# The last two pieces of a mixture-of-experts feed-forward: where the down products of the final slices are issued

## The chip, the cores and the metric

The kernel runs on one NeuronCore of one Trainium2 chip. The metric is the device time of one execution, in microseconds. Before the change the median of three runs was 898.97 us (898.81 to 903.04). The profile is that of one further execution, which took 899.19 us; its records span 897.3 us, so 1.9 us of that time lie outside the span.

## The reference

For 16 batches of 128 tokens, 512 features each, the reference adds a cross attention (32 query heads, 8 key and value heads, head size 16) to the input, and then a feed-forward with 32 experts. A gate picks 8 experts for each of the 2048 tokens, and the feed-forward is

```python
g = jnp.einsum('td,eid->tei', x, w1)
u = jnp.einsum('td,eid->tei', x, w3)
a = jax.nn.silu(g) * u
routed = jnp.einsum('tei,edi,te->td', a, w2, comb)
sh = jax.nn.silu(x @ shared_w1.T) * (x @ shared_w3.T) @ shared_w2.T
out = routed + sh
```

with D = 512 and I = 256, all in float32. Here "up" is the product with w1 or w3, "down" the product with w2.

## The kernel before, in words

Everything up to the experts (attention, the second layer norm, the gate, the shared expert) is left as it is. The routed part sorts the chosen (token, expert) pairs by expert into one long list of 138 slices of 128 rows, numbered 0 to 137. Each expert has a fixed stretch of the list, its capacity (`CAPS`); unused places hold a token number out of bounds, which a transfer skips. A **piece** is one expert's stretch or half of it. The first and the last expert in the list are cut into two pieces each and computed "directly" (`direct`, `up`: four steps, of four matmuls each in the program, one for w1 and one for w3 for each half of I); the experts between them (`fast`) are computed in seven products (`seven`). The last places of the list are these, from the capacities of 448 rows of the last two experts:

| stretch of the list | slices |
|---|---|
| last but one expert in the list ("expert 30") | 131, 132, 133 and the first 64 rows of 134 |
| last expert ("expert 31"), first piece, 192 rows | the last 64 rows of 134, and 135 |
| last expert, second piece, 256 rows of which 248 are computed | 136, 137 |

For a slice `j`, `down(j)` (lines 1714 to 1735) issues the matmuls of the product with w2 into a bank of PSUM, one bank for even slices and one for odd ones. Slice 134 holds rows of two experts, so its matmuls come as two halves of 64 columns, with two weights. One step later `evict(j)` (line 1739) copies the bank on ScalarE, scaled by the gate's weight, into one of four `yw` buffers, and `send` (line 1695) has GpSimd issue an indirect transfer that adds the 128 rows to the output in HBM. Two experts can hold the same token, so the first send of an expert waits until all sends of the expert before it have landed (`add_manual_dep` in `send`, line 1710). A slice with rows of two experts is sent twice: at once for the first expert, and for the second (`token2`) at the head of the next slice's eviction, through the list `waiting`. In this document the two sends of slice 134 are called 134a (expert 30) and 134b (expert 31).

What the engines are given is an order written out by the Python loop over `pieces`. Each step of a piece issues an up product; `tick()` runs the jobs due at that step (evictions, SiLU, products of the gates); and after a step, as many down products are issued as `planned` lists for it, if the slice's time has come: the list `ready_downs` holds pairs of a slice and the step from which it may be issued. A slice joins the list when the piece after its own begins, with a delay `lag`: 3 steps after a fast piece, 1 after a direct one. `many = max(len(ready_downs) - KEPT, 0)` with `KEPT = 1` spreads all but one over the piece's steps. A planned slice that isn't ready goes to the next step. What is left after the last piece is issued in a row. Each engine's queue runs in this order.

Of the kernel before, what the change touches and what calls it, by code (L numbers as in the profile page):

```python
# [46 lines left out]
def tile_xattn_moe(  # L47
# [978 lines left out]
    def experts(ups, in_order, later, products):  # L1026
# [383 lines left out]
        pieces = []  # L1410
# [70 lines left out]
        def block_copies(js):  # L1481


            runs = []
            for q in range(4):
                for j in js:
                    for n, a, b, col in parts(j):
                        if a <= q * Q < b:
                            r, to = j % NB_BUF, col - a
                            last = runs[-1] if runs else None  # L1490
                            if (
                                last
                                and last[0] == q
                                and last[1] == n
                                and last[2] + last[4] == r
                                and last[3] + last[4] * P == to
                            ):
                                last[4] += 1
                            else:
                                runs.append([q, n, r, to, 1])  # L1500
            for q, n, r, to, many in runs:
                for c in range(4):
                    of = blocks[q * Q : (q + 1) * Q, r : r + many, :]
                    of = of.rearrange("p s (k c j) -> p s k c j", c=4, j=Q)[:, :, :, c, :]
                    dst = xnT[n % NTB][c * Q : (c + 1) * Q]
                    at = min(max(to, 0), TB - many * P)
                    dst = dst[:, :, at : at + many * P]
                    dst = dst.rearrange("p k (s t) -> p s k t", t=P)
                    dst = dst[:, :, :, to + q * Q - at : to + (q + 1) * Q - at]
                    on_ACT = c != q or q % 2 == 0  # L1510
                    copy = nc.scalar.copy if on_ACT else nc.vector.tensor_copy
                    yield on_ACT, 1 + many, lambda dst=dst, of=of, copy=copy: copy(dst, of)  # L1512

        def transpose(j):
            nc.vector.transpose(blocks[:, j % NB_BUF, :], xgs[:, j % NG_BUF, 0:D])  # L1515
            weigh(j)
# [51 lines left out]
        def weight_sums(k):  # L1568


            a11, a12, a21, a22 = (
                wup[k % NW][:, :, d : d + 2, ts(i, P)] for i in range(2) for d in (0, 2)
            )
            s1, s2, s4 = (
                late.tile([P, 2, 2, P], F32, tag=name, name=name) for name in ("s1", "s2", "s4")
            )
            sums[k] = s1, s2, a21, s4
            return [
                lambda o=o, a=a, b=b, op=op: nc.vector.tensor_tensor(o, a, b, op)
                for o, a, b, op in (  # L1580
                    (s1, a21, a22, ALU.add),
                    (s2, s1, a11, ALU.subtract),
                    (a21, a11, a21, ALU.subtract),
                    (s4, a12, s2, ALU.subtract),
                )
            ]
# [12 lines left out]
        def token_sums(n):  # L1599


            h = width(n) // 2
            b11, b12, b21, b22 = halves_of(n)
            t1, t2, t4 = (
                late.tile([P, 2, M], F32, tag=name, name=name)[:, :, 0:h]
                for name in ("t1", "t2", "t4")
            )
            tsums[n] = t1, t2, b12, t4
            for out_, a, b in ((t1, b12, b11), (t2, b22, t1), (b12, b22, b12), (t4, b21, t2)):
                yield lambda o=out_, a=a, b=b: nc.vector.tensor_tensor(o, a, b, ALU.subtract)  # L1610
# [142 lines left out]
        def gather_next():  # L1753
            nonlocal n_gathered
            while n_gathered < NS and (n_gathered < NG_BUF or n_gathered - NG_BUF in weighed):
                gather(n_gathered)
                n_gathered += 1
# [8 lines left out]
        def slices_of(n):  # L1766

            end = pieces[n][2]
            return -(-end // P), end // P
# [9 lines left out]
        KEPT = 1  # L1779
        blocks = late.tile([P, NB_BUF, D], F32, name="blocks", bufs=1)  # L1780

        def fast(k):
            return 0 < k < E - 1

        def direct(n):
            banks = {}
            for step in range(4):
                up(n, step // 2, step % 2, banks)
                yield

        def tick():
            nonlocal now
            for f in jobs.pop(now, []):
                f()

        n_copied = n_turned
        ready_downs = []
        for n in range(len(pieces)):
            k = pieces[n][0]
            steps = 7 if fast(k) else 4  # L1800
            ending = n + 1 == len(pieces) or pieces[n + 1][0] > k
            last_piece = len(pieces) - 1

            if n:
                lag = 3 if fast(pieces[n - 1][0]) else 1
                whole = slices_of(n - 1)[1]
                ready_downs += [(j, now + lag) for j in range(n_down, whole)]
                n_down = whole
            many = max(len(ready_downs) - KEPT, 0)
            planned = [(2 * i + 1) * steps // (2 * many) for i in range(many)]  # L1810

            by_PE = range(0)
            if n == 0:
                by_PE = range(n_turned, slices_of(1)[0])
                n_copied = n_turned = slices_of(1)[0]
            on_DVE, on_ACT = [], []
            if ending and fast(k + 1):
                on_DVE += [(4, f) for f in weight_sums(k + 1)]
            if n < last_piece and fast(pieces[n + 1][0]):
                on_DVE += [(3, f) for f in token_sums(n + 1)]  # L1820
            turning = [
                (5, lambda j=j: transpose(j))
                for j in range(n_turned, slices_of(min(n + 3, last_piece))[0])
            ]
            n_turned = max(n_turned, slices_of(min(n + 3, last_piece))[0])
            to_copy = range(n_copied, slices_of(min(n + 2, last_piece))[0])
            n_copied = to_copy.stop
            assert n_turned - to_copy.start <= NB_BUF
            copying = list(block_copies(to_copy))
            if n == 0:  # L1830
                on_DVE += turning[: len(to_copy)]
                del turning[: len(to_copy)]
            on_ACT += [(c, f) for a, c, f in copying if a]
            on_DVE += [(c, f) for a, c, f in copying if not a]
            on_DVE += turning
            dues = [1.0 + 1.5 * planned.count(step) for step in range(steps)]
            done = 0.0
            sides = [(side, sum(c for c, _ in side)) for side in (on_DVE, on_ACT)]
            lefts = [total for _, total in sides]
            for step, _ in enumerate(seven(n) if fast(k) else direct(n)):  # L1840
                tick()
                done += dues[step]
                if step == 1 and by_PE:
                    turn(by_PE)
                for i, (side, total) in enumerate(sides):
                    due = done / sum(dues)
                    if n == 0:
                        due = max(0.0, 2 * due - 1) if i else min(1.0, 2 * due)
                    while side and lefts[i] > total * (1 - due) + 0.01:
                        c, f = side.pop(0)  # L1850
                        f()
                        lefts[i] -= c
                for _ in range(planned.count(step)):
                    if ready_downs and ready_downs[0][1] <= now:
                        down(ready_downs.pop(0)[0])
                    elif step + 1 < steps:
                        planned.append(step + 1)
                gather_next()
                now += 1
            for side, _ in sides:  # L1860
                for _, f in side:
                    f()
                side.clear()
            if ending and k + NW < E:
                load_weights(k + NW, True, False)
# [11 lines left out]
    pieces = [(k, i) for k in range(NTB) for i in range(NI)]  # L1877
    left_over = attention_small()
    experts(pieces[1:], in_order, *left_over)
    left = nc.values_load(  # L1880
        more[0:1, 0:1],
# [63 lines left out]
```

## Time and profile before

| what | value |
|---|---|
| median of three runs | 898.97 us (898.81 to 903.04) |
| profiled execution: its time, its span | 899.19 us, 897.3 us |
| TensorE (PE) busy | 871.5 us, 97% of the span |
| VectorE (DVE), ScalarE (ACT), GpSimd (POOL) busy | 638.9, 641.0, 506.8 us |
| the sends, line 1695 | 150 of them, mean 1619 ns on POOL, 242.8 us in all |
| median from issue to landing of a send | 5.1 us |
| mean TensorE clock granted | 0.993 of full speed |

Times in the timeline count from the start of the span. PE is the matmul side of TensorE, PEld its weight loads, POOLq or SPq the sequencer of an engine. A send's time on POOL is not that of its transfer; the time to landing is listed apart. One matmul of the program stands as two or more matmuls in the trace[...].

### The profile page before, as it was taken

How to read it: one execution, taken by the hardware profiler on the slowest of the kernel's cores; microseconds unless marked ns; L12 is line 12 of the kernel's file. 1: busy time of each engine (PE TensorE's matmuls, PEld its weight loads, DVE VectorE, ACT ScalarE, POOL GpSimd, SP SyncE). 2: the span in 40 equal slices, each digit the busy share in tenths (PEclk: the TensorE clock that was granted, in tenths of full speed). 3: DMA queues.
4: the chain of work that ended last, by engine and by line, in shares of the span. 5: the costliest groups of instructions: out<-in, count | busy, mean ns of one | idle time of the engine just before them, and what ended most of it. 6: DMA issues, size and time to landing. Idle time of an engine off the chain costs nothing. (4 is left out here: it accounts for less than half of the span.)

```text
span 897.3 us, 15744 instructions
## 1 busy us (share of the span) xinstructions
PE 871.5 (97%) x5055; PEld 606.6 (68%) x5055; DVE 638.9 (71%) x1739; ACT 641.0 (71%) x1338; POOL 506.8 (56%) x622
## 2 busy tenths in 40 slices
PE   8999999999899999999999999999999999999993
PEld 4344444555677877778787878787877777777771
DVE  7877768884778767777777777777897777676310
ACT  5888722331989868787989887888896877886531
POOL 3587642575556546555556565656665665644443
PEclk9999999999999999999999999999999999999998
DMA  9111112416578786778787888788877787776443
GB/s 318 39 48 49 50 46 99 149 63 220 165 157 199 156 201 158 173 166 205 168 201 177 187 181 182 180 188 176 213 180 188 202 218 164 162 171 136 85 59 38
DMA packets 59884, 137.28 MB, mean 153 GB/s; under 512 B 12168, under 2 KB 16392, under 8 KB 59792
## 3 DMA queue, kind: packets, MB, share of 16 engines
q0 software_dynamic: 32032, 69.25, 40.3%
q1 hardware_dynamic: 27680, 66.81, 22.0%
q8 instruction: 42, 0.69, 0.3%
q14 instruction: 50, 0.41, 0.2%
q10 hardware_dynamic: 80, 0.13, 0.0%
HBM read 96.71 MB, written 46.73 MB: 160 GB/s over the span
## 5 line engine op out<-in xcount | busy, mean ns | idle before, releaser
L1695 POOL DMA_INDIRECT out_dram<-yw,token x150 | 242.8, 1619 | 226.7 <-ACT yw L1739 134.3
L1512 ACT COPY xnT<-blocks 32x256 f32<-32x256 f32 (+3 forms) x843 | 358.6, 425 | 12.7 <-DVE blocks L1515 0.8
L1723 PE MATMUL y<-wdn,sa 128*128 128x512 f32 (+2 forms) x672 | 259.7, 594 | 0.0
L1615 PE MATMUL p<-xnT,wup 128*128 128x192 f32 (+26 forms) x1152 | 189.6, 311 | 2.8 <-ACT p L1657 2.8
L1432 POOL DMA_INDIRECT xgs<-rows,token x138 | 149.5, 1083 | 68.8 <-DVE own L1524 22.4
L1615 PEld LDWEIGHTS p<-xnT,wup 128*128 128x128 f32 x1152 | 170.3, 191 | 25.9 <-issue 15.4
L1739 ACT ACTIVATE yw<-y,wt 128x512 f32<-128x512 f32 x138 | 94.9, 688 | 107.1 <-PE y L1723 68.3
L1723 PEld LDWEIGHTS y<-wdn,sa 128*128 128x128 f32 (+2 forms) x672 | 96.0, 171 | 73.1 <-issue 70.3
L1615 PEld LDWEIGHTS p<-t,s 128*128 128x128 f32 x768 | 116.6, 191 | 26.5 <-issue 23.0
L1615 PE MATMUL p<-t,s 128*128 128x128 f32 (+26 forms) x768 | 126.6, 310 | 0.9 <-DVE t L1610 0.9
L1515 DVE STREAM_TRANSPOSE blocks<-xgs 128x512 f32<-128x512 f32 x134 | 94.7, 707 | 5.4 <-DMA out_dram<-x 4.9
L1643 DVE TENSOR_TENSOR z<-u,p 128x256 f32<-128x256 f32 (+26 forms) x96 | 48.5, 505 | 41.4 <-PE p L1615 41.2
L1615 PEld LDWEIGHTS p<-t,wup 128*128 128x128 f32 x384 | 59.4, 190 | 19.4 <-issue 12.4
L475 ACT ACTIVATE p<-sc 128x1024 f32<-128x1024 f32 x64 | 62.1, 1023 | 13.7 <-PE sc L465 13.6
L1643 DVE TENSOR_TENSOR u<-u,p 128x256 f32<-128x256 f32 (+26 forms) x48 | 24.4, 509 | 57.5 <-PE p L1615 57.5
L1615 PE MATMUL p<-xnT,s 128*128 128x128 f32 (+26 forms) x384 | 64.3, 310 | 0.0
L1615 PE MATMUL p<-t,wup 128*128 128x128 f32 (+26 forms) x384 | 64.0, 310 | 0.0
L260 PE MATMUL gu<-xnT,sup 128*128 128x512 f32 x128 | 60.7, 616 | 0.7 <-ACT ssl L268 0.7
L1615 PEld LDWEIGHTS p<-xnT,s 128*128 128x128 f32 x384 | 57.2, 191 | 6.1 <-issue 4.5
L1006 POOL TENSOR_SCALAR hq<-slice_q,sq 128x138 f16<-128x138 f16 x32 | 35.2, 1113 | 38.0 <-DVE sq L1314 21.8
L1610 DVE TENSOR_TENSOR t<-xnT,t 128x256 f32<-128x256 f32 (+26 forms) x96 | 48.8, 509 | 0.9
L465 PE MATMUL sc<-qT,kz 32*128 32x512 f32 x256 | 44.2, 639 | 0.5 <-ACT p L475 0.2
(216 smaller groups left out, 1002.0 us busy)
## 6 DMA issues: line engine op xcount, KB each, us to landing
wup<-in_w_dram SPq DMA_DIRECT2D x64, 512.0 KB, 6.1
wdn<-in_w_dram SPq DMA_DIRECT2D x32, 512.0 KB, 4.5
rows<-xn SPq DMA_DIRECT2D x16, 256.0 KB, 2.0
out_dram<-x SPq DMA_DIRECT2D x16, 256.0 KB, 3.0
x<-in_x_dram SPq DMA_DIRECT2D x15, 256.0 KB, 5.8
out_dram<-yw,token POOLq DMA_INDIRECT x150, 5.1
xgs<-rows,token POOLq DMA_INDIRECT x138, 5.0
cTs<-in_cT_dram SPq DMA_DIRECT2D x4, 256.0 KB, 4.5
```

The source lines that it names most:

```text
L260: nc.tensor.matmul(acc, lhsT=sup[:, w, d, ts(i, P)], rhs=xnT[k][:, d, :], start=(d == 0), stop=(d == ND - 1),)
L465: nc.tensor.matmul(scs[j // 2][:, j % 2], lhsT=kzs[b // 4 % 2][rows, b % 4, i, :], rhs=qT[rows], start=True, stop=True, tile_position=(j * ...
L475: nc.scalar.activation(p, sc, AF.Exp, scale=1.0 / HD**0.5)
L1432: nc.gpsimd.indirect_dma_start(out=t, out_offset=None, in_=rows[:, :], in_offset=bass.IndirectOffsetOnAxis(ap=token[:, j : j + 1], axis=0) ...
L1512: yield on_ACT, 1 + many, lambda dst=dst, of=of, copy=copy: copy(dst, of)
L1515: nc.vector.transpose(blocks[:, j % NB_BUF, :], xgs[:, j % NG_BUF, 0:D])
L1610: yield lambda o=out_, a=a, b=b: nc.vector.tensor_tensor(o, a, b, ALU.subtract)
L1615: nc.tensor.matmul(acc[:, i, 0:h], lhsT=w[:, i, d, :], rhs=x[:, d, :], start=(first and i == d == 0), stop=(i == d == 1), skip_group_check ...
L1643: soon(lambda: nc.vector.tensor_tensor(out_, a, b, ALU.add))
L1695: ins = nc.gpsimd.indirect_dma_start(out=flat, out_offset=bass.IndirectOffsetOnAxis(ap=token2[:, k - 1 : k] if a else token[0:b, j : j + 1 ...
L1723: nc.tensor.matmul(y[c0:c1, :], lhsT=acts[n % NTB][:, i, col : col + c1 - c0], rhs=wdn[pieces[n][0] % NW][:, i, :], start=(i == 0), stop=( ...
L1739: nc.scalar.activation(yws[j], y, AF.Copy, scale=wt[:, j : j + 1])
```

## The change

Three edits, all in the loop over the pieces:

```diff
-                lag = 3 if fast(pieces[n - 1][0]) else 1
+                lag = 3 if fast(pieces[n - 1][0]) else 0
...
-            many = max(len(ready_downs) - KEPT, 0)
+            many = max(len(ready_downs) - KEPT, 0) if n < last_piece - 1 else 0
...
+                if n >= last_piece - 1:
+                    planned += [step] * 2
                 for _ in range(planned.count(step)):
+                    if n == last_piece and len(ready_downs) == 1:
+                        break
                     if ready_downs and ready_downs[0][1] <= now:
                         down(ready_downs.pop(0)[0])
```

The slices of a direct piece may be issued from the first step of the next piece. In the last two pieces nothing is spread: each step may issue two slices, and those it can't issue are passed to the next step on top of that step's own two. In the last piece one ready slice is held back until after the piece.

The order of down products (by slice) and up steps on TensorE becomes:

| | before | after |
|---|---|---|
| behind the last step of piece 31, first half | 131, 132 | 131, 132, 133 |
| behind step 0 of the last piece | nothing | 134 |
| behind step 1 | 133 | nothing |
| behind steps 2 and 3 | nothing | nothing |
| after the pieces | 134, 135, 136, 137 | 135, 136, 137 |

The number of matmuls, evictions and sends is the same, and so is the order of the sends among themselves. On ScalarE the eviction of 133 moves ahead of the first SiLU of the last piece, and that of 134 ahead of the second. Nothing moves on VectorE, GpSimd and SyncE, and nothing anywhere ahead of piece 31.

## The prediction

> **What bounds the kernel now.** The page gives TensorE 97% of the span, so I first asked whether the change takes work from it. It doesn't: the same matmuls run in another order. So the end of the program decides, and I read the chain that ended last, in order of time (start, length, what):
>
> ```profile
> 885.84 0.41 issue
> 886.25 2.66 POOLq L1941
> 888.90 0.30 issue
> 889.21 1.57 POOL out_dram L1695
> ```
>
> The chain ends on GpSimd, not on TensorE, with the 150th send. The timeline of the last 20 us (start, length, engine, operation, count, idle time before it and what ended it) says how it gets there:
>
> ```profile
> 876.46 7.29 PE L1723 MATMUL y<-wdn,sa 128*64 128x512 f32 x20
> ...
> 879.48 1.44 POOL L1695 DMA_INDIRECT out_dram<-yw,token  x1 [3.74 <-ACT yw L1739]
> ...
> 880.40 0.69 ACT L1739 ACTIVATE yw<-y,wt 128x512 f32<-128x512 f32 x1 [1.19 <-PE y L1723]
> ...
> 882.12 0.69 ACT L1739 ACTIVATE yw<-y,wt 128x512 f32<-128x512 f32 x1 [1.03 <-PE y L1723]
> ...
> 883.60 1.56 POOL L1695 DMA_INDIRECT out_dram<-yw,token  x1 [2.68 <-DMA out_dram<-yw,token]
> 883.83 0.69 ACT L1739 ACTIVATE yw<-y,wt 128x512 f32<-128x512 f32 x1 [1.03 <-PEq L1886]
> 885.47 1.57 POOL L1695 DMA_INDIRECT out_dram<-yw,token  x1 [0.30 <-issue]
> 887.34 1.56 POOL L1695 DMA_INDIRECT out_dram<-yw,token  x1 [0.30 <-issue]
> 889.21 1.57 POOL L1695 DMA_INDIRECT out_dram<-yw,token  x1 [0.30 <-issue]
> ```
>
> In the first line slices 134 to 137 run in a row and TensorE ends at 883.75. The sends are 134a (879.48), then 134b (883.60) after 2.68 us idle for a transfer, then 135, 136, 137, each 1.87 us after the one before (1.57 and 0.30 of issue). Slices 135 and 136 were evicted by 881.1 and 882.8, yet went out at 885.47 and 887.34: they stood behind 134b, and 134b stood for the landing of 134a. That landing is in the view of the sends that start between 879 and 880 us:
>
> ```profile
> DMA to landing us min/median/max: 3.3/3.3/3.3
> ```
>
> So 134a lands at 879.48 + 3.3 = 882.78, and 134b starts 0.82 us later. The other landings, looked up likewise, are 4.8, 6.2, 5.0 and 3.3 us from the start of 134b, 135, 136, 137: the last falls at 889.21 + 3.3 = 892.5. After the sends comes line 1941, the end of the program (count, shortest/median/longest in ns, first and last start in us):
>
> ```profile
> L1941 SPq EVENT_SEMAPHORE  x12: 27/28/28, 888.4 to 893.0; - x12
> ...
> L1941 POOLq DRAIN  x1: 10247/10247/10247, 886.2 to 886.2; - x1
> ...
> L1941 ACTq DRAIN  x1: 80/80/80, 887.7 to 887.7; - x1
> ```
>
> SyncE has seen all landings by 893.0, ScalarE and TensorE are through at 887.8, and GpSimd's drain runs to 886.25 + 10.25 = 896.5, which is 5.7 us after the last send ended (890.78) and 4.0 after the last landing (892.5). Only 0.8 us of barrier follow to 897.3. The end thus hangs on the last send, and the last send on the landing of 134a.
>
> **What the Trainium skill says.** "Perfetto Trace Analysis", section "DMA Instruction — SWDGE (GPSIMD)": the profiled end of such a send is the end of descriptor generation, and the movement of data lies outside it. This trace agrees: 1.57 us on POOL, 3.3 to 6.2 us to landing. "DMA: Bandwidth & Descriptors", section "Rules for kernel authors": an accumulating transfer has to wait for the semaphore of an earlier one to the same bytes. The wait of 134b is of that kind, 2.68 us idle here. The same page, section "Anatomy of one DMA — SWDGE (gpsimd) path", gives about 2.0 us fixed per transfer, mostly the confirmation of the write; the sparse send 134a took 3.3 us here, so I use the trace's number.
>
> **The change, step by step.** A full down product takes 4 trace matmuls of 0.43 us, 1.72 us (871.30 to 873.02 for slice 133). Two up steps of the last piece take 16 trace matmuls, 3.34 us (867.96 to 871.30), so one takes 1.67. Slice 134 takes 1.87 (876.46 to 878.33), with 0.10 ahead of it: the up steps before it took 3.44 instead of 3.34.
>
> *TensorE.* The first point that differs is behind slice 132; 131 starts at 864.52. After: 131 to 133 take 3 × 1.72 = 5.16, to 869.68; step 0 takes 1.67, to 871.35; with the 0.10, 134 starts at 871.45 and ends its issue at 873.32; three up steps take 5.01, to 878.33. Then comes 135, and it starts at 878.33 in the trace of before too. So TensorE's end stays; the edit costs nothing there unless a moved product waits. Slice 134 needs the bank of 132 (evicted by about 868.9), the activations of piece 31's first half (last product on VectorE at 864.79 + 0.35 = 865.14) and expert 31's w2 (its load was issued at 849.61; the page's median to landing is 4.5 us): 2.6 us or more of slack in each. Slice 136 needs the last gate product, 878.33 + 0.17 + 0.41 = 878.9 by the pattern at 876.47 to 877.05; held-back 135 covers it until 880.05. Without that cover 136 would start some 0.6 us late.
>
> *ScalarE.* An eviction starts about 0.2 to 0.35 us after its product and takes 0.69. The one of 133 now stands ahead of the first SiLU (869.88 to 870.57; the SiLU's input is ready at 871.4), the one of 134 ahead of the second (873.5 to 874.2; input ready at 876.7). Neither holds a SiLU up: cost nothing. The buffers they write belong to sends 129 and 130, issued at 858.82 and 861.79 and landed by about 865.
>
> *GpSimd.* A send starts 0.96 us after its eviction starts if the engine is free (866.44 to 867.40, and 878.52 to 879.48). 131 and 132 stay at 867.40 and 869.26; 133 comes at 871.13. 134a: eviction at 871.45 + 2.06 (876.46 to 878.52 before) = 873.5, send at 874.46, landing 3.3 later at 877.76, and 134b 0.82 later at 878.6, done at 880.15: wholly beneath the last up steps. 135: evicted from 880.40 as before, sent at 880.40 + 0.96 = 881.36. 136: the later of 882.12 + 0.96 = 883.08 and 881.36 + 1.87 = 883.23. 137: the later of 884.79 and 883.23 + 1.87 = 885.10.
>
> | | before | after, estimate |
> |---|---|---|
> | 134b starts | 883.60 | 878.6 |
> | last send starts | 889.21 | 885.10 |
> | last send ends | 890.78 | 886.67 |
> | POOL's drain ends (+5.7) | 896.5 | 892.4 |
> | span | 897.3 | 893.2 |
>
> The gain is 4.11 us: 2.24 us in which 135 stood for the landing of 134a, and 1.87 for 134b itself in front of it. What is late next is the chain 135's product, eviction, three sends; 137's own eviction would allow 884.79, only 0.31 earlier. Against the profiled execution's 899.19 that is 895.1; the median of the runs lies 0.22 lower, so I forecast 898.97 − 4.1 = **894.9 us**.
>
> *The unknown.* The trace doesn't show what the drain of GpSimd waits for. If for the last send, it moves by 4.11. If for the last landing, it moves by what the landings move: with 135 no longer behind a fresh transfer, 136 takes 4.7 to 5.3 (the pair at 867.40 and 869.26 showed these) and lands at 887.9 to 888.5, 137 at 885.10 plus 2.8 to 3.3 (2.8 is the shortest of the tail), 887.9 to 888.4, so the last landing is at 887.9 to 888.5 against 892.5: a gain of 4.0 to 4.6. I take 4.1, and keep 3.8 and 4.8. A loss is excluded unless a landing grows, below.
>
> **The rivals.**
> *The same chain, worth more.* The landings come early as just worked out, and TensorE saves 0.1 to 0.3 us on fewer waits between banks: a gain of 4.5 to 5.0, near 894.3. For it: four sends in a row before had landings up to 6.2 us, so contention was there. Against: with the drain tied to the send, nothing of it counts.
> *The wait is only shortened.* 134a now goes out 3.3 us behind 133 and may land late. With 6.2 us, the longest of this tail, 134b starts at 874.46 + 6.2 + 0.82 = 881.48 and the last send at 887.09: a gain of 2.1, 896.9 us. Against: up to 4.2 us nothing is lost, and 134a is short of rows (9 GB/s in its slice of the trace, against 119 for 133).
> *The other side.* The same wait, longer: the last send starts at 874.46 + L + 0.82 + 3 × 1.87 = 880.89 + L, with L the landing of 134a. From L = 8.3 the change loses; at L = 13 it costs 4.7, 903.7 us. No landing in the tail is beyond 6.2.
> *It does nothing.* GpSimd's drain is held by something that doesn't move, and the time stays at 899.0. Against: no other engine has anything left after 887.8 but SyncE's waits for these landings.
>
> **How the numbers follow.** About 0.5% (4.5 us) is what a measurement of this kernel can tell from no change, and my 4.1 lies close beneath. The main case has 0.62, with its own range 894.3 to 895.4, and 0.12 of it beyond the line; worth more 0.24; shortened 0.05; nothing 0.04; slower 0.05. Faster by over 0.5%: 0.12 + 0.24 = 0.36. Within: 0.50 + 0.05 + 0.04 = 0.59. Slower: 0.05. The range 893.8 to 896.9 takes the main case, most of the larger one and the shortened one, and leaves out the last two and the tail of the second.
>
> **What would show it.** In the profile after: 134b starts near 878.6 and ends before the last products; no idle time for a transfer ahead of 135; the last three sends at about 881.4, 883.2 and 885.1; TensorE's last down products from 878.3 to 883.7; the drain's end 5.7 us after the last send. I am wrong if 134 starts much after 871.5 (a moved product waits), if 134b still starts after 880, or if the drain's end doesn't follow.

## The result, and the profile after

The changed kernel takes 894.98 us in the median of 17 runs; the kernel before, in 17 runs beside them, 899.99. The measured ratio, which is not the plain quotient of these two medians (0.9944), is 0.9949 with a 95% interval of 0.9935 to 0.9962; a second measurement on another occasion gave 0.9959 (0.9940 to 0.9978). The forecast was 894.9 us. One run of the changed kernel took 2306.47 us and is left out of the ratio, and the other runs of each kernel fall into two groups 3 to 4 us apart (one run of before, 899.99, lies between); the medians of the faster groups are 898.88 and 894.79 us, 4.09 us apart.

The profiled executions took 899.19 us (span 897.3) and 894.69 us (span 892.9), 4.5 us apart; of these 0.37 us lie ahead of the first point where the two programs differ, since slice 131 starts on TensorE at 864.52 before and at 864.15 after. To keep such offsets out (among the executions below they reach 4 us, as much as the gain itself), most times of this section are also counted from the start of slice 131.

First the timeline of the changed kernel, the lines that answer to those of before:

```profile
871.07 1.94 PE L1723 MATMUL y<-wdn,sa 128*64 128x512 f32 x8
...
874.09 1.44 POOL L1695 DMA_INDIRECT out_dram<-yw,token  x1 [1.78 <-ACT yw L1739]
...
878.06 5.31 PE L1723 MATMUL y<-wdn,sa 128*128 128x512 f32 x12
878.17 1.56 POOL L1695 DMA_INDIRECT out_dram<-yw,token  x1 [2.65 <-DMA out_dram<-yw,token]
...
880.03 0.69 ACT L1739 ACTIVATE yw<-y,wt 128x512 f32<-128x512 f32 x1 [3.06 <-PE y L1723]
...
880.99 1.56 POOL L1695 DMA_INDIRECT out_dram<-yw,token  x1 [1.25 <-ACT yw L1739]
...
882.86 1.56 POOL L1695 DMA_INDIRECT out_dram<-yw,token  x1 [0.30 <-issue]
883.46 0.69 ACT L1739 ACTIVATE yw<-y,wt 128x512 f32<-128x512 f32 x1 [1.03 <-PEq L1890]
884.73 1.57 POOL L1695 DMA_INDIRECT out_dram<-yw,token  x1 [0.30 <-ACTq L1890]
```

Slice 134 now runs at 871.07, and 134a goes out at 874.09. GpSimd still idles 2.65 us for its landing ahead of 134b (878.17), about as long as before (2.68), but TensorE is still at work then: 135 to 137 start at 878.06. When 135 has been evicted, 134b is out, and what ended the 1.25 us of idle time ahead of 135 is its own eviction. The wait for the transfer was not removed; it was moved beneath TensorE.

The chain that ended last, for the same stretch (start, length, what), shows it in order; the last three sends in it are those of the timeline:

```profile
874.09 3.30 DMA out_dram<-yw,token
...
878.17 1.56 POOL out_dram L1695
879.74 1.02 issue
...
884.73 1.57 POOL out_dram L1695
```

The landing of 134a took 3.30 us. The chain counts nearly all of the time between 879.74 and 880.99 as issue; the timeline names the wait for 135's eviction there. Less the 0.30 us that lie between any two sends in a row, this is the slack of the transfer, 0.95 us. The end of the program (line 1945 in the changed file, columns as before):

```profile
L1945 SPq EVENT_SEMAPHORE  x12: 28/28/28, 882.8 to 888.7; - x12
...
L1945 POOLq DRAIN  x1: 6530/6530/6530, 885.5 to 885.5; - x1
```

GpSimd's drain ends at 885.48 + 6.53 = 892.01, which is 5.72 us after the last send's end (886.29), as before (890.78 to 896.50, 5.72).

| from the start of slice 131 | before | after | difference |
|---|---|---|---|
| 134a starts | 14.96 | 9.94 | 5.02 |
| 134b starts | 19.08 | 14.02 | 5.06 |
| 135 sent | 20.95 | 16.84 | 4.11 |
| last send starts | 24.69 | 20.58 | 4.11 |
| TensorE ends | 19.23 | 19.23 | 0.00 |
| drain of GpSimd ends | 31.98 | 27.86 | 4.12 |

### The profile page after: what moved, and what is told of

Its sections match the earlier page's. It is cut to its first block, busy times and chain, and to the rows that moved or that the text cites. A ratio compares the mean times of both kernels' runs of the same rounds, so it can differ in the third digit from the quotient of the medians.

```text
span 892.9 us, 15745 instructions
## 1 busy us (share of the span) xinstructions
PE 872.7 (98%) x5055; PEld 608.4 (68%) x5055; DVE 639.3 (72%) x1739; ACT 640.9 (72%) x1338; POOL 505.4 (57%) x622
## 4 chain that ended last, share of the span: by engine, by line
PE 93%; issue 2%; POOL 1%; ACT 1%; DVE 1%; DMA 1%; POOLq 0%; ACTq 0%; DVEq 0%
PE p L1615 44%; PE y L1723 25%; PE gu L260 6%; PE sc L465 5%; PE oT L481 3%; PE y L1348 3%; PE x L435 2%; PE gu L1546 2%; POOL out_dram L1695 1%; PE tok L1012 1%; DMA out_dram<-yw,token 1%; PE warm L331 1%; PE lgT L542 0%; PE lg L557 0%; ACT p L475 0%
## 5 line engine op out<-in xcount | busy, mean ns | idle before, releaser
L1432 POOL DMA_INDIRECT xgs<-rows,token x138 | 146.8, 1063 | 70.3 <-issue 25.4
```

The source lines that it names most:

```text
L1432: nc.gpsimd.indirect_dma_start(out=t, out_offset=None, in_=rows[:, :], in_offset=bass.IndirectOffsetOnAxis(ap=token[:, j : j + 1], axis=0) ...
```

## The experiments

Two theories on the gain. **W**, that of the prediction: the end hangs on GpSimd's chain of sends, and the gain is the wait for 134a's landing plus the slot of 134b. **T**: the new order on TensorE is worth the time by itself. And on what closes the program: **S**, the drain follows the last send; **L**, it follows the last landing; **P**, it follows whatever GpSimd did last.

### Slice 134 one step later

```diff
-                lag = 3 if fast(pieces[n - 1][0]) else 0
+                lag = 3 if fast(pieces[n - 1][0]) else 1
```

> The changed kernel with the delay of a direct piece back at 1 step, so that slice 134 is issued behind step 1 of the last piece instead of step 0, 1.67 us later on TensorE; all else as changed. Times on the scale of the changed kernel's trace (slice 131 starts at 864.15, last send at 884.73, span 892.9). Theory W (the end hangs on the chain 134a, its landing, 134b, 135, 136, 137): 134a starts at 874.09 + 1.67 = 875.76, lands 3.3 later, 134b starts at 879.84 and leaves GpSimd free at 881.70; 135 starts there instead of at 880.99, so 0.71 us of the 1.67 come through, the last send starts at 885.44 and the span is 893.6. Rival T (the gain comes from TensorE, whose down products now stand in fewer, longer rows): TensorE ends where it did, the span stays at 892.9 within 0.2.

Measured: span 892.6, time 894.32 (one run). GpSimd's lines:

```profile
875.46 1.44 POOL L1695 DMA_INDIRECT out_dram<-yw,token  x1 [3.45 <-ACT yw L1739]
878.80 1.56 POOL L1695 DMA_INDIRECT out_dram<-yw,token  x1 [1.90 <-DVE sa L1560]
880.69 1.56 POOL L1695 DMA_INDIRECT out_dram<-yw,token  x1 [0.33 <-ACT yw L1739]
```

134a comes 1.67 us later as expected (11.61 from the start of slice 131). But 134b follows it after 3.34 us where it took 4.08 in the changed kernel and 4.12 before. The timeline puts the end of 134b's idle time down to an operation of VectorE that was over at 878.44; the chain of this execution has the landing of 134a there, 2.55 us after its start, in place of 3.30:

```profile
875.46 2.55 DMA out_dram<-yw,token
```

So GpSimd is free at 880.66, just in time for 135, and the last send is at 20.58, as in the changed kernel. The expected loss of 0.71 us is 0: the landing was 0.75 us shorter. Taken alone this run speaks for T as much as for W; it shows that the time to the landing of 134a varies. In the executions here, 134b (or 135 where 134b was left out) starts 3.33 to 4.12 us after 134a.

### Slice 134 two steps later

```diff
-                lag = 3 if fast(pieces[n - 1][0]) else 0
+                lag = 3 if fast(pieces[n - 1][0]) else (2 if n == last_piece else 0)
```

> The same with a delay of 2 steps into the last piece: slice 134 behind step 2, 3.34 us later than in the changed kernel. Theory W: 134a at 877.43, 134b at 881.51, 135 at 883.37, last send at 887.11, 2.38 us later than in the changed kernel, span 895.3, time about 897.4, some 1.7 us under the kernel before. Rival T: 892.9, time 895.0.

Measured: median 896.29 us, ratio to the kernel before 0.9969 (0.9958 to 0.9981).

```profile
879.65 1.44 POOL L1695 DMA_INDIRECT out_dram<-yw,token  x1 [5.12 <-ACT yw L1739]
882.98 1.56 POOL L1695 DMA_INDIRECT out_dram<-yw,token  x1 [1.89 <-DMA out_dram<-yw,token]
884.85 1.57 POOL L1695 DMA_INDIRECT out_dram<-yw,token  x1 [0.30 <-ACT yw L1739]
```

Now 135 is sent 1.87 us after 134b, with no slack left: it stands behind it again. Slice 131 starts at 866.37 here, so 134a is 3.34 us later than in the changed kernel, 135 and the last send (22.22) 1.64 later. W gave 2.38 with a distance of 4.08 between 134a and 134b; with the 3.33 of this execution it gives 2.38 − 0.75 = 1.63. T gave nothing. The sequence step 0, step 1, step 2 and the place after the pieces gives 20.58, 20.58, 22.22 and 24.69 for the last send: flat as long as the slack lasts, then rising with the delay. With the short landings of these two runs the slack is 0.95 + 0.75 = 1.70 us: it covers the delay of 1.67, and of the 3.34 it leaves 1.64.

### The kernel before without its second send of slice 134

```diff
         def send(j, k, a, b):
+            if j == NS - 4 and a:
+                return
```

> The kernel before, with the order of TensorE untouched, without send 134b (the rows of the last expert in slice 134 are not added to the output). 135 then waits for the landing of 134a in its place. Theory W: the slot of one send falls away, 1.87 us: 135 starts at 883.60, the last send at 887.34 instead of 889.21, span 895.4, time 897.1. Rival T: 897.3 and 899.0, unchanged.

Measured: median 896.72, ratio 0.9979 (0.9969 to 0.9990). The send of 135:

```profile
885.86 1.57 POOL L1697 DMA_INDIRECT out_dram<-yw,token  x1 [2.54 <-ACT yw L1741]
```

The eviction that the view names was over by 883.50, so the idle time ended with something else; that it is the landing of 134a follows from the next run, where the wait is gone together with that send. Slice 131 starts at 866.94; 134a at 881.90 (14.96, as before); 135 at 885.86, 3.96 us later; the last send at 889.59, 22.65 from the start of slice 131 instead of 24.69. That is 2.04 us: the slot of 1.87, and 0.16 because the start after 134a's came at 3.96 instead of 4.12. T is not consistent with it: TensorE's order is that of before.

### The kernel before without both sends of slice 134

```diff
         def send(j, k, a, b):
+            if j == NS - 4:
+                return
```

> The kernel before without both sends of slice 134 (none of its rows is added to the output). 135 then waits for the landing of 133 only (874.18 + 4.7 = 878.9, before its own eviction). Theory W: the wait and the slot both fall away, 2.24 + 1.87 = 4.11 us, as in the change: 135 at 881.36, last send at 885.10, span 893.2, time 894.9, although TensorE runs the order of before. Rival T: 897.3 and 899.0, unchanged.

Measured: median 894.67, ratio 0.9953 (0.9939 to 0.9966).

```profile
880.12 7.29 PE L1725 MATMUL y<-wdn,sa 128*64 128x512 f32 x20
...
884.06 0.69 ACT L1741 ACTIVATE yw<-y,wt 128x512 f32<-128x512 f32 x1 [1.19 <-PE y L1725]
885.02 1.56 POOL L1697 DMA_INDIRECT out_dram<-yw,token  x1 [5.62 <-ACT yw L1741]
```

TensorE still runs 134 to 137 in a row (880.12, 7.29 us), as in the kernel before, and yet 135 is sent 0.96 us after its eviction starts: 16.83 from the start of slice 131, where the changed kernel has 16.84, and the last send at 20.56 against 20.58. The order on TensorE is worth nothing of its own; T falls. Wait and slot together are 24.69 − 20.56 = 4.13 us, the whole of the change's 4.11. The times agree with the traces in the last three runs: the last send moves by 2.47, 2.04 and 4.13 us against the kernel before, 0.27, 0.23 and 0.46% of 899, and the ratios give 0.31, 0.21 and 0.47%.

### Without the slice held back

```diff
-                    if n == last_piece and len(ready_downs) == 1:
-                        break
```

> The changed kernel without the slice held back: 134 and 135 both behind step 0, only 136 and 137 after the last up step. Times on the scale of the changed kernel's trace. As the prediction put it, 136 waits some 0.6 us for the last gate product without the cover of 135: TensorE ends 0.6 us later, 137 is evicted from 884.0, sent at 885.0, 0.3 later than in the changed kernel, span 893.2. Rival: the first half of 136's own matmuls (0.86 us) needs only the first gate product and covers the wait; TensorE doesn't stop, 136 is sent at 882.71 and 137 at 884.58, 0.15 earlier than in the changed kernel, span 892.7.

Measured: span 892.6, time 894.45 (one run). The timeline of TensorE, VectorE and ScalarE:

```profile
874.65 5.18 PE L1546 MATMUL gu<-xnT,wup 128*128 128x248 f32 x24
...
879.67 3.60 PE L1723 MATMUL y<-wdn,sa 128*128 128x512 f32 x8
879.94 0.41 DVE L1560 TENSOR_TENSOR sa<-sg,gu 128x248 f32<-128x248 f32 x1 [2.93 <-PE gu L1546]
880.41 0.31 PEld L1723 LDWEIGHTS y<-wdn,sa 128*128 128x128 f32 x2 [0.55 <-DVE sa L1560]
881.64 0.69 ACT L1739 ACTIVATE yw<-y,wt 128x512 f32<-128x512 f32 x1 [3.06 <-PE y L1723]
```

The weight load that reads the last gate product does wait, 0.55 us, but behind two trace matmuls of the same slice that need only the first gate product: 136 starts at 879.67 without a stop and is evicted at 17.59 from the start of slice 131 (17.60 in the changed kernel). TensorE ends at 19.22 (19.23). 135's send moves out of the end, 136 goes at 18.55 and 137 at 20.42, 0.16 earlier than in the changed kernel; the rival of this expectation had 0.15. The drain ends 0.15 earlier, too little for the times to show. The third edit is not needed here.

### What the drain waits for: without the last send

```diff
         def send(j, k, a, b):
+            if j == NS - 1:
+                return
```

> The changed kernel without the send of slice 137 (its rows are not added to the output). Theory S (GpSimd's drain ends 5.75 us after the last send's end on GpSimd): the last send is 136's, from 882.86 to 884.42, the drain ends at 890.2, span 891.0, 1.87 less. Theory L (the drain ends some 4 us after the last landing): 136 lands at about 887.9 and 137 at about 888.0 in the changed kernel, so the end moves by 0.1 to 0.3 us only, span 892.6 to 892.8.

Measured: span 895.5, with slice 131 at 867.23. The last send, now 136's, starts at 885.93 and ends at 887.49. The view of that send, and the end of the program (line 1947 there):

```profile
DMA to landing us min/median/max: 5.7/5.7/5.7
```

```profile
L1947 POOLq DRAIN  x1: 7807/7807/7807, 886.8 to 886.8; - x1
```

The drain ends at 886.84 + 7.81 = 894.64, 27.41 from the start of slice 131 against 27.86: 0.45 us earlier. S alone gave 1.87 and is refuted as the only condition, L gave 0.1 to 0.3. It is 7.15 us after the send's end, and 3.0 after that send's landing (885.93 + 5.7 = 891.6). So there is a second condition, hidden in the two kernels compared. Before, the last landing is at 892.5. After, the trace gives no landing of the last sends; SyncE's last wait starts at 888.7, and before it started at 893.0, 0.5 behind the last landing, so 888.2 is an estimate. 3.0 us on top of these (895.5 and 891.2) stays 0.8 to 1.0 us below the drains' ends.

### What the drain waits for: work of GpSimd behind the sends

```diff
         for args in waiting:
             send(*args)
+        for _ in range(2):
+            nc.gpsimd.tensor_scalar(
+                blocks[:, 0, 0:256], blocks[:, 0, 0:256], 1.0, 0.0, ALU.mult, ALU.add
+            )
```

> The changed kernel with two operations of GpSimd on 128x256 float32 behind the last send, which touch nothing that is still used; from the 1.1 us of a 128x138 operation some 2 us each, an estimate, so that they end at about 890.5. Theory P (the drain ends 5.75 us after whatever GpSimd did last): drain to 896.3, span 897.1. Theories S and L (it ends after the last send or the last landing): drain and span unchanged, 892.05 and 892.9.

Measured: span 896.3, with slice 131 at 865.73 (30.6 us to the span's end, against 28.7).

```profile
886.30 1.57 POOL L1695 DMA_INDIRECT out_dram<-yw,token  x1 [0.31 <-ACTq L1894]
887.94 0.89 POOL L1879 TENSOR_SCALAR blocks<-blocks 128x256 f32<-128x256 f32 x2
```

```profile
L1879 POOL TENSOR_SCALAR blocks<-blocks x2: 405/405/405, 887.9 to 888.4; 128x256 f32<-128x256 f32 x2
```

```profile
L1949 POOLq DRAIN  x1: 5778/5778/5778, 889.7 to 889.7; - x1
```

The operations took 0.41 us each, not the estimated 2; the 0.89 of the timeline is the length of the pair. They end at 887.94 + 0.89 = 888.83, and the drain at 889.67 + 5.78 = 895.45, which is 1.86 us later from the start of slice 131 than in the changed kernel (29.72 against 27.86). The last send alone would give 887.87 + 5.72 = 893.59, and the last landing (890.1) plus 3.0 us 893.1. So work behind the sends does move the end, in the direction of P, but P's size failed: the drain ends 6.62 us after the last operation, not 5.75. What comes close is the drain's own start. It lies behind the operations here (889.67), and the drain lasts 5.78 from it; in the two kernels it lies ahead of the last send's end (886.25 and 890.78 before, 885.48 and 886.29 after). "5.72 to 5.78 us after the later of the drain's start and the last send's end" covers all three, but one run alone has the order turned round, and the profile's times on GpSimd are rough, so what exactly the drain counts from stays open.

### What the drain waits for: later landings

```diff
+        r = (E - 1) % NW
+        for dst, src in (
+            (wup[r][:, 0], w1),
+            (wup[r][:, 1], w3),
+            (xnT[last_piece % NTB][:, 0:2, :], w1),
+            (xnT[last_piece % NTB][:, 2:4, :], w3),
+        ):
+            nc.sync.dma_start(
+                dst.rearrange("p a b -> p (a b)"),
+                src[0:1].rearrange("o p a b -> (o p) (a b)"),
+            )
         ready_downs += [(j, 0) for j in range(n_down, NS)]
```

> The changed kernel with four more loads of 512 KB on SyncE's queue into buffers that are free after the last up products, so that 2 MB flow from about 876.5 to 886 beside the last sends: their landings come 1 to 3 us later, their starts on GpSimd do not (135, 136, 137 don't wait for each other's landings). Theory S: the drain still ends 5.75 us after the last send's end, near 892.05, span 892.9. Theory L: it moves with the last landing, 893 to 895, span 894 to 896.

Measured: span 895.9, with slice 131 at 866.56. The last send starts at 887.14 (20.58, as in the changed kernel) and ends at 888.70; its landing, and the end of the program:

```profile
DMA to landing us min/median/max: 4.9/4.9/4.9
```

```profile
L1956 POOLq DRAIN  x1: 7158/7158/7158, 887.9 to 887.9; - x1
```

The landings of 135, 136 and 137 take 6.8, 6.4 and 4.9 us, where the run with slice 134 one step later has 5.2, 5.4 and 4.1. The last falls at 887.14 + 4.9 = 892.0, and the drain ends at 887.89 + 7.16 = 895.05: 6.35 us after the send, 3.0 after the landing. So where the sends are GpSimd's last work, the drain's end is the later of two: 5.72 us after the end of the last send, and 3.0 us after the last landing of a send. The kernel before without 134b lies near the border: the rule gives 897.0 by its last landing (893.99) and 896.88 by its last send, and 896.98 was measured.

### The changed kernel again, and a try at the rest of the chain

> The changed kernel itself once more, to be compared with the next one on the same chip. From the start of slice 131 on TensorE: last send 20.58 us later, GpSimd's drain ends 27.86 us later, by the rule that the runs so far give (the later of 5.72 us after GpSimd's last instruction and 3.0 us after the last landing). Ratio to the kernel before between 0.994 and 0.996.

Measured: median 894.97, ratio 0.9959 (0.9940 to 0.9978); last send 20.57 after the start of slice 131, drain 27.86. GpSimd's last instruction is the last send here.

The try no longer holds a slice back and shares the last two evictions:

```diff
-            nc.scalar.activation(yws[j], y, AF.Copy, scale=wt[:, j : j + 1])
+            if j < NS - 2:
+                nc.scalar.activation(yws[j], y, AF.Copy, scale=wt[:, j : j + 1])
+            else:
+                h = D // 2
+                nc.scalar.activation(
+                    yws[j][:, 0:h], y[:, 0:h], AF.Copy, scale=wt[:, j : j + 1]
+                )
+                nc.vector.tensor_scalar(
+                    yws[j][:, h:D], y[:, h:D], wt[:, j : j + 1], None, ALU.mult
+                )
...
-                    if n == last_piece and len(ready_downs) == 1:
-                        break
```

> The changed kernel without the slice held back, and with the evictions of 136 and 137 shared, half of the columns on ScalarE and half on VectorE, some 0.4 us each instead of 0.69 (the SiLU of 128x248 takes 0.38, VectorE's product of 128x248 0.41). From the start of slice 131: 136 sent 0.3 earlier than without the hold alone, at 18.27, 137 at 20.14 instead of 20.58; the drain ends 5.72 us after that send's end, at 27.43 instead of 27.86. 0.4 us, which the trace can show and the times cannot. If the rule is wrong and the drain follows the landings, it ends at 27.3 to 27.9.

Measured: median 895.10, ratio 0.9953 (0.9936 to 0.9970), no difference that the times can show. The trace says that the idea did not come about:

```profile
881.93 0.48 ACT L1743 ACTIVATE yw<-y,wt 128x256 f32<-128x256 f32 x1 [3.06 <-PE y L1723]
882.44 0.48 DVE L1746 TENSOR_SCALAR yw<-y,wt 128x256 f32<-128x256 f32 x1 [1.79 <-ACT yw L1743]
883.20 1.56 POOL L1695 DMA_INDIRECT out_dram<-yw,token  x1 [2.15 <-DVE yw L1746]
```

VectorE's half starts when ScalarE's has ended: in this program the second access to the same pair of tiles waits for the first. Two halves in a row take 0.99 us where the whole took 0.69, 136 is sent at 18.86 where 18.27 was expected and 137 at 20.73 where 20.14 was, 0.31 us later than in the run that only left out the hold (18.55 and 20.42). The drain ends at 28.01, again 5.72 us after the last send's end.

## Why the prediction was right, point by point

- **What bounds the kernel.** Right, and shown: with TensorE's order untouched, taking away the two sends of slice 134 gives the whole gain (4.13 us of last send, ratio 0.9953).
- **TensorE's end stays.** Right: 135 starts 13.91 us after slice 131 in the changed kernel, predicted 878.33 − 864.52 = 13.81, and TensorE's end is at 19.23 in both.
- **"Without that cover 136 would start some 0.6 us late."** Wrong. The wait of 0.55 us is there, but the first half of 136's own matmuls covers it. The step missed that the first half of a down product reads only the first gate product, and that only its second half waits for the second. The forecast of 4.11 us doesn't contain it.
- **The chain of sends.** Predicted 134a 9.94, 134b 14.08, 135 16.84, last send 20.58 us after slice 131's start; measured 9.94, 14.02, 16.84, 20.58. The gain of 4.11 at the last send was met to 0.01 us in the trace. That the wait would stay and only be covered was part of it, and is what the profile shows.
- **The landing of 134a.** The 3.3 us held in the profiled execution of the changed kernel (the chain has 3.30). That they were met so closely is luck, since other executions have 2.5 to 2.9 and the distance to the next start is 3.33 to 4.12 us; the gain did not hang on it, as anything up to 4.2 us stays covered. A shorter landing, 2.55 us, is why a delay by one step cost nothing where 0.71 us was expected.
- **The unknown of the drain.** The value taken, that it moves with the last send, was right for this change, but in part by luck: the prediction had no means to choose between the send and the landing. Both conditions exist, and the one on the last send came last in both kernels, by 0.8 to 1.0 us.
- **The rivals.** "Worth more" failed at the step it named: the landings did come earlier, SyncE is through at 888.7 instead of 893.0, but nothing followed from it, and TensorE saved nothing. "Shortened", "the other side" and "nothing" did not occur; the run with slice 134 two steps later shows the loss that the first of them named, 1.64 us at the last send once the slack is used up, though there 134a starts late and its landing is short.
- **The size in per cent.** The trace's 4.11 us are 0.46% of 899; the times gave 0.51% and 0.41%, with intervals that hold 0.46%. Both intervals also hold 0.5%, so on which side of that line the gain lies is not decided. That 894.9 lies 0.1 us beside the measured median is partly luck: the median of before moved by 1.0 us between 3 and 17 runs, and the two medians are 5.0 us apart where 4.1 was forecast.

## What to carry to other kernels

Where an engine is 97% busy, look at what still runs when it stops: here 13.6 us of the span lay behind TensorE's last matmul, and the chain there, not TensorE's work, decided what a reordering was worth. A transfer that others must wait for belongs early enough that its landing falls beneath the busy engine; beyond the point where it is covered, moving it further gained nothing here (step 0 against step 1). Before giving work a cover against a wait, look whether the waiting operation's own first half already covers it.

## What was not expected of the hardware

- The end of the program on GpSimd took 5.72 us after the last send's end in the kernel before and in the changed one, unless the last landing plus 3.0 us was later (3.0 us in the runs without the last send, with later landings and, near the border, without 134b). With two plain operations behind the sends it took 6.62 us from the end of the second, and 5.78 from the drain's own start. In both kernels compared the 5.72 us are the longest single part of what follows TensorE's end.
- The same transfer of a half-filled slice took between about 2.5 us (slice 134 one or two steps later) and 3.3 us (before and after) to land in executions of almost the same program, and the send that waited for it started 0.7 to 0.8 us after the landing.
